# A four-layer graph network kernel: softmax moved down the scheduler's list in the last layer, the layer's end written out, the last output in two pieces

## The chip, the cores and the metric

The kernel runs on one core of a Trainium2 chip. The metric is the device time of one execution in microseconds; several executions were timed and their median is given. One more execution was taken with the hardware profiler; all views and line numbers come from that one.

## The reference

The input x is 128 graphs of 64 nodes with 256 features, float32. Four layers follow each other, each of the form x = x + layer(relu(layernorm(x))). Layers 0 to 2 (two graph convolutions and windows of small LSTMs) are not touched by the change. The last layer is attention over E = 512 edges (src, dst) with 4 heads of 64:

```python
Xq = (H @ W_lin.T).reshape(bt, n, h, dh)
Xv = (H @ W_val.T).reshape(bt, n, h, dh)
e = jnp.einsum('behd,hd->beh', jax.nn.leaky_relu(Xq[:, src] + Xq[:, dst], 0.2), a)
e = e + jnp.log(A0[src, dst] + EPS)[None, :, None]
# softmax of e over the edges of one src node: minus segment_max, exp, over segment_sum
Y = jax.ops.segment_sum(attn[..., None] * Xv[:, dst], src, num_segments=n)
return Y @ W_out.T
```

## The kernel before, in words

The 8192 rows (128 graphs x 64 nodes) stand in SBUF as 16 blocks X[0] to X[15] of 512 rows. The last layer works in groups of four graphs: 32 groups, g = 0 to 31, two groups to a block. Edges are sorted by src and kept as one-hot matrices, so that gathers and segment sums become matmuls: ed_S (src plus dst, one-hot), OST (src, transposed) and ODT (dst, transposed). Eight groups share one score tile "acc" of 128 x 512 (128 rows of graph and head, 512 edges), so softmax is made once for eight groups, after g = 7, 15, 23 and 31.

The steps, with the names that the profile shows:

- turned (L2473): normalizes a block (norm), transposes it on TensorE (ps<-ident,h) and copies the two halves out (hT), one on VectorE, one on ScalarE.
- queries (L2483): four matmul chains hT x (W_lin | W_val), each into one PSUM buffer "ps" of 512 columns (ps<-w_qv,hT). ScalarE copies the first 256 columns out (Q), VectorE the other 256 (XV). Then VectorE forms the linear part of the leaky relu: a product (lin_p) and two reductions (lin).
- score (L2507): eight matmuls Q x ed_S for a group (ps<-ed_S,Q), each into a "ps" buffer, and eight relus on ScalarE (r).
- reduce (L2520): sums r over features with the vector a into acc (acc<-r,ed_apad). The first group of eight starts acc with the log of the adjacency (acc<-ed_log,ones).
- softmax (L2575): calls shifted (L2587): one more matmul adds lin to acc (acc<-ed_S,lin); two scans over the edges give the running maximum per src node from both sides; maximum, subtraction (sm_e), Exp on ScalarE. Then two more scans sum the exponentials per node, with a masking step between them, and a reciprocal and a product give the attention e. All but Exp and the matmul are on VectorE.
- edgewise (L2601), two groups later: transposes e (ps<-ident,sm_e) and copies it into "at".
- between (L2613) calls spread (L2618): four VectorE products at x OST into "aw" buffers (five of them), and gathered (L2629): matmuls aw x ODT into "ps" (ps<-aw,ed_ODT) and one ScalarE copy to "an".
- weighted (L2640): 32 small matmuls an x XV (y<-an,XV) into one PSUM pair of banks, and two copies to "y".
- output (L2656): y x W_out (ps<-w_o,y), VectorE adds it to X (X<-X,ps), and the SyncE queue writes the 256 KB to HBM.
- back (L2227), for g < 8: adds what layer 2 left for a later block (ps<-ident,ls_t).

PSUM in this layer has five "ps" buffers, one "acc" and one pair for y (L2420). Attention runs ten groups behind score (LAG = 10, v = g - 10).

What sets the order: the steps are written in one Python loop (L2434 to L2463), and the tile framework's scheduler lays each engine's instructions out ahead of time. It walks through its own estimate of time and gives an engine, whenever that is free there, the ready instruction that was written first. So the order in the source is a list of priorities and not the order itself. On the chip each engine then takes its instructions in the order laid out. For a group with softmax the list was: score(g), weighted, reduce(g), edgewise, between, **softmax**, turned (next block), back, output, queries (next block). 

The last softmax (q = 3, after g = 31) is written out by hand in turn (L2533): while nc.ordered is set (class Ordered, L788), every instruction on TensorE, VectorE and ScalarE is tied behind the one written before it on the same engine; DMAs are not. In turn, the sums of the exponentials per node come from matmuls with OST (ps<-sm_m,ed_OST), their reciprocals (ed_contr) are spread back by matmuls (ps<-ed_contr,ed_cont), and "at" is the product of the two (at<-sm_m,ps). Groups 22 and 23 are gathered meanwhile, and outputs 20 to 23 made. After turn, a loop (L2465) does between, weighted and output for the last eight groups, with the scheduler choosing the order.

Of the kernel before, what the change touches and what calls it, by code (L numbers as in the profile page):

```python
# [8 lines left out]
F32 = mybir.dt.float32  # L9
# [14 lines left out]
class Ops:  # L24
# [9 lines left out]
    def add(self, o, a, b):  # L34
        self.tt(o, a, b, ALU.add)
# [40 lines left out]
class Eig:  # L76
# [156 lines left out]
    def split(self, D, E):  # L233
# [57 lines left out]
        o.ts(neg[:], ae[:], -1.0, ALU.mult)  # L291
        W, w = t("W", 2), t("w", 1)
        nc.vector.memset(W[:], 0.0)
        for x in range(3):
# [3 lines left out]
            o.mul(ez[:], ez[:], O[:, x, :])  # L298
            col = W[:, 1:2] if x == 1 else W[:, 0:1]
            o.ts(w[:], self.P[:], B1[:, x + 1:x + 2], ALU.is_equal, 0.5 ** 0.5, ALU.mult)  # L300
# [32 lines left out]
        o.stt(self.t("junk4", 4)[:], NB[:], 1.0, self.LM[:], ALU.mult, ALU.mult, acc=n[:])  # L333
        Ws = self.mm(PT[:], W[:])
        WS = t("WS", 2)
# [577 lines left out]
class Fast:  # L913
# [276 lines left out]
    def poly(self, X, each):  # L1190

        o, nc, t = self.o, self.nc, self.t
        PB = t("PB", 128, 33, 64)
        W = t("W", 128, 64)
        o.ts(PB[:, 1, :], X, self.DD[:, 0:1], ALU.subtract)
        for s in range(1, 32):
            o.stt(W[:], X, self.DD[:, s:s + 1], PB[:, s, :], ALU.subtract, ALU.mult)
            o.stt(PB[:, s + 1, :], PB[:, s - 1, :], self.E2[:, s:s + 1], W[:], ALU.mult, ALU.add)
# [244 lines left out]
B, N, D = 128, 64, 256  # L1443
P = 128
# [5 lines left out]
NG = 4  # L1450
# [15 lines left out]
class Kernel:  # L1466
# [949 lines left out]
    def layer3(self):  # L2416
        nc, o, io = self.nc, self.o, self.io
        cx, (w,) = self.stage([("l3x", 1)], "tile")
        with cx:
            cy, pools = self.stage([("l3", 2), ("l3v", 2), ("l3s", 1), ("l3r", 6), ("l3ps", 5), ("l3cps", 1), ("l3yps", 1)], "tile")  # L2420
            with cy:
                self.a02 = self.everywhere(w, "ed_a", io["L3_gnn_a"].rearrange("h d -> (h d)"))
                o.ts(self.a02[:], self.a02[:], 0.2, ALU.mult)
                self.drop, self.dropr = (w.tile([P, E], F32, name="ed_" + n) for n in ("drop", "dropr"))
                o.ts(self.drop[:], self.cont[:], 1.0, ALU.subtract, FLOOR, ALU.mult)
                o.ts(self.dropr[:], self.contr[:], 1.0, ALU.subtract, FLOOR, ALU.mult)
                WQV = w.tile([P, 2, 2 * D], F32, name="w3_qv")
                for x, n in enumerate(("W_lin", "W_val")):
                    nc.sync.dma_start(WQV[:, :, x * D:(x + 1) * D],
                                      io[f"L3_gnn_{n}_t"].rearrange("(k p) m -> p k m", p=P))  # L2430
                WO = self.weights(w, "w3_o", io["L3_gnn_W_out_t"])


                st, LAG = {}, 10  # L2434
                self.turned(st, 0, *pools)
                self.queries(st, 0, WQV, *pools)
                for g in range(8 * NG):
                    v = g - LAG
                    ahead = (g + 1) // 2 if g % 2 and g + 1 < 8 * NG else None
                    self.score(st, g, *pools)  # L2440
                    if v >= 1:
                        self.weighted(st, v - 1, *pools)
                    self.reduce(st, g, *pools)
                    if g % 8 == 1 and 1 < g:
                        self.edgewise(st, g // 8 - 1, *pools)
                    if v >= 0:
                        self.between(st, v, *pools)
                    if g % 8 == 7 and g + 1 < 8 * NG:
                        self.softmax(st, g // 8, *pools)
                    if ahead:  # L2450
                        self.turned(st, ahead, *pools)
                    if g < 8:
                        self.back(8 + g, pools[4], "ps")
                    if g + 6 == 8 * NG:

                        p = pools[4].tile([P, BT], F32, name="ps")
                        for c in range(4):
                            self.nc.tensor.transpose(p[:N, c * P:(c + 1) * P], self.OST[:, c, :], self.ident[:])
                        self.act_copy(self.cont[:N, :], p[:N, :])
                    if v >= 1 and g + 1 < 8 * NG:  # L2460
                        self.output(st, v - 1, WO, *pools)
                    if ahead:
                        self.queries(st, ahead, WQV, *pools)  # L2463
                self.turn(st, WO, pools)
                for v in range(8 * NG - 8, 8 * NG + 2):  # L2465
                    if v < 8 * NG:
                        self.between(st, v, *pools)
                    if 8 * NG - 8 < v <= 8 * NG:
                        self.weighted(st, v - 1, *pools)
                    if v > 8 * NG - 7:  # L2470
                        self.output(st, v - 2, WO, *pools)

    def turned(self, st, i, pool, vp, sp, rp, psum, psc, psy):  # L2473

# [58 lines left out]
    def turn(self, st, WO, pools):  # L2533


        nc, o, psum = self.nc, self.o, pools[4]
        q, v = NG - 1, 8 * NG - 10
        nc.ordered = True
        W = [self.spread(st, v, c, *pools) for c in (0, 2)]
        e, m, m2 = self.shifted(st, q, *pools)  # L2540
        self.output(st, v - 2, WO, *pools)
        self.gathered(st, v, W, *pools)
        et = m2[:].rearrange("p (c b) -> p c b", c=4)
        p = psum.tile([P, 4, P], F32, name="ps")
        for c in range(4):
            nc.tensor.transpose(p[:, c, :], e[:, c * P:(c + 1) * P], self.ident[:])
        self.act_copy(et, p[:])
        self.weighted(st, v - 1, *pools)
        W = [self.spread(st, v + 1, 0, *pools)]
        p = psum.tile([P, P], F32, name="ps")  # L2550
        for c in range(4):
            self.mm(p[:N, :], self.OST[:, c, :], et[:, c, :], c == 0, c == 3)

        sums = self.contr[:N, 0:P]
        o.ts(sums, p[:N, :], 0.5, ALU.max)
        o.recip(sums, sums)
        self.output(st, v - 1, WO, *pools)
        W.append(self.spread(st, v + 1, 2, *pools))
        self.gathered(st, v + 1, W, *pools)
        at = st["at", q] = pools[1].tile([P, 4, 2, 8, 2, HEADS], F32, name="at")  # L2560
        p = psum.tile([P, 4, P], F32, name="ps")
        for c in range(4):
            self.mm(p[:, c, :], self.cont[:N, c * P:(c + 1) * P], sums)
        for x in range(2):
            for m in range(2):
                z = 64 * x + 32 * m
                by = lambda t: t[:, :, z:z + 32].rearrange("p c (a h) -> p c a h", h=HEADS)
                o.mul(at[:, :, x, :, m, :], by(et), by(p))
        self.weighted(st, v, *pools)
        self.output(st, v, WO, *pools)  # L2570
        self.weighted(st, v + 1, *pools)
        nc.ordered = False
        self.output(st, v + 1, WO, *pools)

    def softmax(self, st, q, pool, vp, sp, rp, psum, psc, psy):  # L2575

# [7 lines left out]
        o.mul(e[:], e[:], m2[:])  # L2584
        st["e", q] = e

    def shifted(self, st, q, pool, vp, sp, rp, psum, psc, psy):  # L2587

        nc, o = self.nc, self.o
        acc, lin = st["acc", q], st["lin", q]  # L2590
        self.mm(acc[:], lin[:].rearrange("p x m a h -> p (x m a h)"), self.S2[:], False, True)
        e, m, m2 = (vp.tile([P, E], F32, name="sm_" + x, bufs=1) for x in ("e", "m", "m2"))
        scan = nc.vector.tensor_tensor_scan
        scan(m[:], self.drop[:], acc[:], -FLOOR, op0=ALU.add, op1=ALU.max)
        scan(m2[:, ::-1], self.dropr[:, ::-1], acc[:, ::-1], -FLOOR, op0=ALU.add, op1=ALU.max)
        o.tt(m[:], m[:], m2[:], ALU.max)
        o.sub(e[:], acc[:], m[:])
        self.act(e[:], e[:], AF.Exp)
        return e, m, m2
# [53 lines left out]
            (self.move if g < 8 * NG - 11 else self.act_copy)(y[:, :, :, x, :].rearrange("p f m s -> p m f s"),  # L2653
                      yp[:, x, 0:4 * N].rearrange("p (m f s) -> p m f s", m=2, f=2))

    def output(self, st, g, WO, pool, vp, sp, rp, psum, psc, psy):  # L2656

        y = st["y", g]
        p = psum.tile([P, 2, D], F32, name="ps")
        for m in range(2):  # L2660
            for f in range(2):
                self.mm(p[:, m, :], y[:, f, m].rearrange("p x s -> p (x s)"), WO[:, f, :], f == 0, f == 1)
        x = self.X[g // 2][:, 2 * (g % 2):2 * (g % 2) + 2, :]
        self.o.add(x, x, p[:])
        out = self.io["out"].rearrange("b n d -> (b n) d")
        self.nc.sync.dma_start(out[2 * g * P:(2 * g + 2) * P, :].rearrange("(t p) d -> p t d", p=P), x)

    def run(self):
        self.begin()
# [54 lines left out]
```

## Time and profile before

| what | value |
|---|---|
| median of 3 runs | 2345.52 us (2345.03 to 2349.55) |
| the profiled execution's own time | 2350.61 us |
| its span, first to last instruction | 2348.8 us |
| TensorE busy | 2298.7 us (98%) |
| VectorE busy | 1590.5 us (68%) |
| ScalarE busy | 1138.2 us (48%) |
| mean granted TensorE clock | 0.994 |
| fourth layer | about 1752 us to the end |
| a plain matmul row of it: ps<-aw,ed_ODT, 128x512 | 512 records, 118.2 us |
| aw product on VectorE, 128x1024 | 1220 ns each, some 1150 from start to start |
| reciprocal of sm_m, 128x512 | 3340 ns each, three of them |

PE is TensorE's matmuls, PEld its weight loads, DVE VectorE, ACT ScalarE, POOL GpSimd, SP SyncE. A float32 matmul is two records. Ends of matmuls are modelled, so the time a block of matmuls takes is best read from its first start to the next block's first start. A bracket at the end of a timeline row gives the idle time of that engine before the row, and what ended it. All rows have the line L799, that of a helper that records the instructions, so rows are told apart by their tiles.

### The profile page before, as it was taken

To read this page: it belongs to the slowest core of one execution; us is meant where nothing else is said; L and a number is where in the kernel's file an instruction comes from. 1 tells how busy PE (TensorE), PEld (TensorE's weight loads), DVE (VectorE), ACT (ScalarE), POOL (GpSimd) and SP (SyncE) were. 2 spreads that over 40 slices of the span, in tenths; PEclk is the share of its full clock that TensorE was granted. 3 is DMA by queue.
4 is the path that set the end of the run, shared out by engine and by line. 5 is a ranking of instruction groups with operands and counts; after the bars stand their busy time and mean duration, and the time that the engine had idled before them with its cause. 6 is when DMAs were issued, how large, how long until landed. Compare 5 with 4: busy or idle time off the path is not lost.

```text
span 2348.8 us, 32636 instructions
## 1 busy us (share of the span) xinstructions
PE 2298.7 (98%) x12173; PEld 1633.1 (70%) x12173; DVE 1590.5 (68%) x3988; ACT 1138.2 (48%) x2503; POOL 2.9 (0%) x26
## 2 busy tenths in 40 slices
PE   7999998999999999999999999999999999999999
PEld 4555446986777788888999998888874444444444
DVE  7877676998447777666767667569655566556457
ACT  4665864654436654444444444347445544334321
POOL 0000000000000000000000000000000000000000
PEclk9999999999999999999999999999999999999999
DMA  5000221130010000001000001000020000000001
GB/s 170 1 1 19 63 60 29 66 89 19 1 36 1 1 19 1 1 1 37 1 1 1 1 8 65 1 1 17 1 72 1 1 5 19 14 15 14 19 19 46
DMA packets 61193, 54.86 MB, mean 23 GB/s; under 512 B 15204, under 2 KB 58853, under 8 KB 61029
## 3 DMA queue, kind: packets, MB, share of 16 engines
q1 hardware_dynamic: 61028, 52.73, 7.3%
q8 instruction: 97, 1.59, 0.3%
q14 instruction: 68, 0.55, 0.1%
HBM read 35.93 MB, written 16.78 MB: 22 GB/s over the span
## 4 chain that ended last, share of the span: by engine, by line
PE 80%; DVE 3%; ACT 1%; issue 0%; DMA 0%; ACTq 0%; DVEq 0%
PE ps L799 69%; PE acc L799 5%; PE pt L799 4%; DVE sm_m L799 1%; PE pe L799 1%; PE y L799 1%; DVE X L799 0%; DVE aw L799 0%; ACT ls_g L799 0%; ACT L799 0%; DMA ls_w<-in_L_gnn_Wih_t_dram 0%; DVE ls_g L799 0%; DVE XV L799 0%; DVE ls_t L799 0%; DVE hT L799 0%
## 5 line engine op out<-in xcount | busy, mean ns | idle before, releaser
L799 ACT ACTIVATE ls_g<-ls_g,ls_b 128x512 f32<-128x512 f32 (+4 forms) x472 | 243.0, 565 | 153.4 <-DVE ls_g L799 151.5
L799 ACT ACTIVATE ls_g<-ps,ls_b 128x256 f32<-128x256 f32 (+3 forms) x268 | 115.4, 470 | 330.4 <-PE ps L799 327.1
L799 PE MATMUL ps<-z,w 128*128 128x512 f32 x512 | 259.0, 630 | 0.9 <-ACT z L799 0.9
L799 DVE TENSOR_TENSOR aw<-at,ed_OST 128x1024 f32<-128x1024 f32 x128 | 149.1, 1220 | 97.4 <-PE ps L799 97.4
L799 PE MATMUL ps<-big,X 128*128 128x176 f32 (+3 forms) x848 | 213.0, 367 | 0.8 <-ACT big L799 0.7
L799 DVE TENSOR_TENSOR ls_g<-ls_z,ps 128x512 f32<-128x512 f32 (+5 forms) x256 | 147.1, 580 | 91.4 <-PE ps L799 90.0
L799 PE MATMUL ps<-ls_tx,X 128*128 128x160 f32 (+2 forms) x960 | 207.1, 327 | 0.6 <-ACT ls_g L799 0.6
L799 PE MATMUL ps<-X,X 128*128 128x160 f32 (+1 forms) x896 | 199.1, 306 | 0.0
L799 PE MATMUL ps<-X,ls_w 128*128 128x256 f32 x640 | 190.5, 379 | 0.0
L799 PEld LDWEIGHTS ps<-ls_tx,X 128*128 128x128 f32 x960 | 161.9, 190 | 15.2 <-DVE X L799 4.9
L799 PEld LDWEIGHTS ps<-big,X 128*128 128x128 f32 x848 | 146.1, 190 | 30.5 <-issue 19.4
L799 DVE TENSOR_TENSOR X<-ls_g 128x1024 f32<-128x1024 f32 (+2 forms) x108 | 117.5, 1088 | 51.1 <-ACT ls_g L799 51.1
L799 ACT ACTIVATE r<-ps 128x512 f32<-128x512 f32 x256 | 129.2, 626 | 43.1 <-PE ps L799 43.1
L799 PEld LDWEIGHTS ps<-X,X 128*128 128x128 f32 x896 | 148.5, 190 | 0.0
L799 PE MATMUL ps<-X,ls_s 128*128 128x256 f32 x480 | 142.3, 379 | 0.0
L799 PEld LDWEIGHTS ps<-z,w 128*128 128x128 f32 x512 | 88.7, 193 | 70.9 <-issue 62.3
L799 PE MATMUL ps<-ls_tx,ls_s 128*128 128x256 f32 x464 | 134.9, 379 | 0.0
L799 PE MATMUL ps<-ls_tx,ls_w 128*128 128x256 f32 x464 | 133.4, 380 | 0.0
L799 PEld LDWEIGHTS ps<-X,ls_w 128*128 128x128 f32 x640 | 121.6, 190 | 16.6 <-DVE X L799 0.3
L799 PE MATMUL ps<-big,ls_w 128*128 128x256 f32 x464 | 132.0, 380 | 0.7 <-ACT ls_z L799 0.7
L799 PE MATMUL ps<-ed_S,Q 64*128 64x512 f32 x512 | 129.6, 617 | 2.3 <-DVE XV L799 2.2
L799 ACT ACTIVATE h<-X,n_m,n_r 128x256 f32<-128x256 f32 x192 | 99.6, 590 | 40.9 <-issue 25.0
(543 smaller groups left out, 4010.4 us busy)
## 6 DMA issues: line engine op xcount, KB each, us to landing
X<-in_x_dram SPq DMA_DIRECT2D x32, 512.0 KB
xs<-X SPq DMA_DIRECT2D x16, 512.0 KB
X<-xs SPq DMA_DIRECT2D x16, 512.0 KB
out_dram<-X SPq DMA_DIRECT2D x32, 256.0 KB
X<-in_L_gnn_Wih_t_dram SPq DMA_DIRECT2D x4, 512.0 KB
ls_w<-in_L_gnn_Wih_t_dram SPq DMA_DIRECT2D x4, 512.0 KB
ls_w<-in_L_gnn_Whh_t_dram SPq DMA_DIRECT2D x4, 512.0 KB
w<-in_L_gnn_W_t_dram SPq DMA_DIRECT2D x2, 512.0 KB
```

The lines of the kernel that those rows point to most:

```text
L799: i = method(*a, **kw)
```

## The change

Four edits, all in the fourth layer. First, the acc matmul of lin moves out of shifted into a step of its own, summed, which stands where softmax stood; softmax itself is now written behind queries. Second, in turn, gathered of group 23 moves behind the matmuls and products that make "at", and the first two aw products of group 24 come ahead of weighted(22). Third, the loop over the last eight groups moves into turn, under nc.ordered, with its order written out: the last two aw products of a group, the add and DMA of the output before the last (late), gathered, the first two aw products of the next group, weighted of the group before, and the matmuls of the output before that. Fourth, output can hand its add and DMA back to be made later, and the last group's output is split into two pieces of 128 rows (two graphs) each, each with its own PSUM buffer, add and DMA.

```diff
@@ layer3
                     if g % 8 == 7 and g + 1 < 8 * NG:
-                        self.softmax(st, g // 8, *pools)
+                        self.summed(st, g // 8, *pools)
                     if ahead:
                         self.turned(st, ahead, *pools)
...
                     if ahead:
                         self.queries(st, ahead, WQV, *pools)
+                    if g % 8 == 7 and g + 1 < 8 * NG:
+                        self.softmax(st, g // 8, *pools)
                 self.turn(st, WO, pools)
-                for v in range(8 * NG - 8, 8 * NG + 2):
-                    if v < 8 * NG:
-                        self.between(st, v, *pools)
-                    if 8 * NG - 8 < v <= 8 * NG:
-                        self.weighted(st, v - 1, *pools)
-                    if v > 8 * NG - 7:
-                        self.output(st, v - 2, WO, *pools)
@@ turn
         W = [self.spread(st, v, c, *pools) for c in (0, 2)]
+        self.summed(st, q, *pools)
         e, m, m2 = self.shifted(st, q, *pools)
...
         W.append(self.spread(st, v + 1, 2, *pools))
-        self.gathered(st, v + 1, W, *pools)
         at = st["at", q] = pools[1].tile([P, 4, 2, 8, 2, HEADS], F32, name="at")
...
                 o.mul(at[:, :, x, :, m, :], by(et), by(p))
+        self.gathered(st, v + 1, W, *pools)
+        W = [self.spread(st, v + 2, 0, *pools)]
         self.weighted(st, v, *pools)
-        self.output(st, v, WO, *pools)
-        self.weighted(st, v + 1, *pools)
+
+        late = lambda: None
+        for v in range(8 * NG - 8, 8 * NG + 2):
+            if v < 8 * NG:
+                W.append(self.spread(st, v, 2, *pools))
+            late()
+            if v < 8 * NG:
+                self.gathered(st, v, W, *pools)
+            if v + 1 < 8 * NG:
+                W = [self.spread(st, v + 1, 0, *pools)]
+            if v <= 8 * NG:
+                self.weighted(st, v - 1, *pools)
+            late = self.output(st, v - 2, WO, *pools, late=True)
+        late()
         nc.ordered = False
-        self.output(st, v + 1, WO, *pools)
@@ softmax, shifted
+    def summed(self, st, q, pool, vp, sp, rp, psum, psc, psy):
+
+        self.mm(st["acc", q][:], st["lin", q][:].rearrange("p x m a h -> p (x m a h)"), self.S2[:], False, True)
+
     def shifted(self, st, q, pool, vp, sp, rp, psum, psc, psy):
-        nc, o = self.nc, self.o
-        acc, lin = st["acc", q], st["lin", q]
-        self.mm(acc[:], lin[:].rearrange("p x m a h -> p (x m a h)"), self.S2[:], False, True)
+        nc, o, acc = self.nc, self.o, st["acc", q]
@@ output
+        parts = []
+        for lo, hi in ((0, 1), (1, 2)) if g == 8 * NG - 1 else ((0, 2),):
+            p = psum.tile([P, 2, D], F32, name="ps")[:, 0:hi - lo, :]
+            for m in range(lo, hi):
+                for f in range(2):
+                    self.mm(p[:, m - lo, :], y[:, f, m].rearrange("p x s -> p (x s)"), WO[:, f, :], f == 0, f == 1)
+            parts.append((p, lo, hi))
+
+        def add():
+            for p, lo, hi in parts:
+                x = self.X[g // 2][:, 2 * (g % 2) + lo:2 * (g % 2) + hi, :]
+                self.o.add(x, x, p)
+                self.nc.sync.dma_start(out[(2 * g + lo) * P:(2 * g + hi) * P, :].rearrange("(t p) d -> p t d", p=P), x)
+
+        if late:
+            return add
+        add()
```

More of the change, by code (lines that the diff above doesn't have):

```diff
@@ L2654, in weighted, with output @@
                       yp[:, x, 0:4 * N].rearrange("p (m f s) -> p m f s", m=2, f=2))
-    def output(self, st, g, WO, pool, vp, sp, rp, psum, psc, psy):
+    def output(self, st, g, WO, pool, vp, sp, rp, psum, psc, psy, late=False):
         y = st["y", g]
[L2659 to L2664, printed above, removed]
-        out = self.io["out"].rearrange("b n d -> (b n) d")
-        self.nc.sync.dma_start(out[2 * g * P:(2 * g + 2) * P, :].rearrange("(t p) d -> p t d", p=P), x)
+        out = self.io["out"].rearrange("b n d -> (b n) d")
+        parts = []
[13 more added lines that the diff above has]
+        add()
     def run(self):
```

## The prediction

> **What bounds the kernel now.** I read the page first, then busy time by stage for the last layer, then the timelines of TensorE (PE) and VectorE (DVE) at the places where the stages are longer than their neighbours. The page's first line says who is short of time.
>
> ```profile
> PE 2298.7 (98%) x12173; PEld 1633.1 (70%) x12173; DVE 1590.5 (68%) x3988; ACT 1138.2 (48%) x2503; POOL 2.9 (0%) x26
> ```
>
> PE is the bound, and the chain of waits agrees (PE 80% of it). So an edit outside PE is worth only what it takes out of PE's gaps. The change touches the fourth layer alone (from about 1752 us). Busy time by stage there (columns: stretch, length, busy us of PE, PEld, DVE, ACT, POOL with instructions, granted PE clock, DMA):
>
> ```profile
> 1814.02:1842.30 28.28, 28.28 (x122) 12.31 (x121) 12.64 (x29) 15.63 (x31) 0.00 (x0) 1.00 0.00 1
> 1838.71:1872.58 33.87, 31.80 (x125) 13.12 (x124) 22.11 (x38) 17.71 (x33) 0.00 (x0) 1.00 0.00 1
> 2081.03:2115.59 34.56, 34.56 (x201) 15.45 (x200) 17.82 (x26) 13.89 (x29) 0.00 (x0) 1.00 0.05 16
> 1969.84:2011.15 41.31, 39.81 (x205) 16.74 (x204) 27.94 (x40) 17.39 (x33) 0.00 (x0) 0.96 0.04 13
> 2115.59:2155.26 39.67, 38.17 (x206) 16.41 (x205) 27.02 (x29) 15.90 (x31) 0.00 (x0) 1.00 0.04 14
> ```
>
> The first and third rows are ordinary pairs of groups: PE has no gap at all. The second, fourth and fifth are the same work plus a softmax (g = 7, 15, 23). They carry two matmul pairs that the ordinary rows don't have (acc<-ed_S,lin, 0.96 us from start to next start, and acc<-ed_log, 1.05): 2.01 us of real work. The rest of the excess is stall: 33.87 - 28.28 - 2.01 = **3.58**; 41.31 - 34.56 - 2.01 = **4.74**; 39.67 - 34.56 - 2.01 = **3.10 us**. What stalls PE at g = 23 stands in the DVE timeline (start, duration):
>
> ```profile
> 2128.93 1.22 DVE L799 TENSOR_TENSOR_SCAN sm_m<-ed_drop,acc 128x512 f32<-128x512 f32 x1
> 2130.06 1.20 DVE L799 TENSOR_TENSOR_SCAN sm_m<-ed_dropr,acc 128x512 f32<-128x512 f32 x1
> 2131.18 0.67 DVE L799 COPY hT<-ps 128x512 f32<-128x512 f32 x1
> ...
> 2138.67 1.22 DVE L799 TENSOR_TENSOR_SCAN sm_m<-ed_contr,sm_m 128x512 f32<-128x512 f32 x1
> 2139.91 3.35 DVE L799 RECIPROCAL sm_m<-sm_m 128x512 f32<-128x512 f32 x1
> 2143.18 0.36 DVE L799 COPY XV<-ps 128x256 f32<-128x256 f32 x1
> ```
>
> and in PE's:
>
> ```profile
> 2131.90 7.13 PE L799 MATMUL ps<-w_qv,hT 128*128 128x512 f32 x16 [0.77 <-DVE hT L799]
> 2138.96 3.91 PE L799 MATMUL ps<-ed_S,Q 64*128 64x512 f32 x14
> 2143.60 1.12 PE L799 MATMUL ps<-ed_S,Q 64*128 64x512 f32 x2 [0.73 <-DVE XV L799]
> ```
>
> Two waits, both on a DVE copy standing behind softmax. First, the hT copy runs after two scans though its transposes were over before the first. Second, the fourth XV copy, which frees one of the five PSUM buffers "ps", runs after the reciprocal; score needs that buffer. The bracketed 0.73 understates the second: score takes 5.69 us from its first start to the next step (2138.96 to 2144.65) against 3.84 in ordinary odd steps, so it costs 1.85.
>
> The other place is the written-out turn at the end:
>
> ```profile
> 2282.26 5.05 PE L799 MATMUL ps<-aw,ed_ODT 128*64 128x512 f32 x16
> 2287.24 1.16 PE L799 MATMUL ps<-ed_contr,ed_cont 64*128 64x128 f32 x8
> 2288.32 0.69 PE L799 MATMUL y<-an,XV 64*64 64x64 f32 x32
> 2289.79 1.99 PE L799 MATMUL ps<-w_o,y 128*128 128x256 f32 x8 [0.78 <-ACT y L799]
> 2291.72 0.69 PE L799 MATMUL y<-an,XV 64*64 64x64 f32 x32
> 2293.19 2.00 PE L799 MATMUL ps<-w_o,y 128*128 128x256 f32 x8 [0.78 <-ACT y L799]
> 2295.11 7.45 PE L799 MATMUL ps<-aw,ed_ODT 128*64 128x512 f32 x32
> ```
>
> Twice an output follows its own y at once and waits for ACT's evacuation, and the first aw block takes 4.98 us to the next start where 3.58 is usual. After 2303 PE is full again, 6.13 us a step. The end:
>
> ```profile
> 2344.64 0.69 DVE L799 TENSOR_TENSOR X<-X,ps 128x512 f32<-128x512 f32 x1 [1.04 <-PE ps L799]
> ```
>
> [...] the 0.36 us copy stands behind the 3.35 us reciprocal. [...] XV copies wait for ACT's Q copy of the same bank (32 waits, 34.0 us), so an XV copy is ready only once its Q is. [...] The trace has such a drop of 3.41 us at 2000.50, just after the g = 15 stalls[...]: acc<-r takes 5.13 us there, 3.48 after g = 23. That is the 1.65 by which the fourth row exceeds the fifth.
>
> **The change, part by part.**
>
> *Softmax behind queries.* Nothing is added or removed; the acc matmul stays (summed), the DVE/ACT chain goes behind turned, back, output and queries in the list. At g = 23 DVE comes free at 2129.0 with hT's transposes done, so hT goes first and ends near 2129.7; PE needs it at 2130.7 (end of the w_o step). The gap goes whole: 1.10 - 0.09 (four y records) + 0.08 (the cut y block) + 0.10 (restart of QV, 7.06 against 6.96) = 1.19. The QV block and all XV copies come 1.1 earlier: the last MM ends near 2137.8, Q near 2138.2, XV ready 2138.3, while the chain reaches its reciprocal no sooner than before (2139.9), since hT, the add and three XV copies stood ahead of it already. XV then has the higher place, so the 1.85 goes too: **3.04** at g = 23 and at g = 15. At g = 7: back block 2.30 against 0.87, 1.43; QV 0.10; score 5.95 against 3.84, 2.11; sum 3.64. Here DVE is idle when acc is ready, so one scan (to 1853.1) still precedes hT: QV at 1853.8 where 1853.5 would be free, 0.3 to 0.4 stays: **3.25**. Sum **9.3**. What becomes late is e: lin_p (1.22) and two reductions (2.44) now pass it, 3.7 us. Its reader, the sm_e transposes, comes at 1880.07 against e at 1867.43 (later groups 19 to 21 us): hidden with over 5 us to spare. Bounds: 0 (reciprocal still ahead) to 9.7.
>
> *The turn.* Steps stay, their order changes: gathered(23) after the cont matmuls, weighted one step ahead of its output. PE's excess now, over 2271.60 to 2307.67: y 0.14 + 0.85 + 0.85, aw 1.40 + 0.22 + 0.34 = 3.80. Afterwards DVE paces it: add at 2282.36 as now, two aw to 2285.33, four at products (0.88) to 2286.1, then aw at 1.15 each from 2286.06. PE: cont 2282.26 to 2283.35; gathered(23) waits 0.25 for its last aw; gathered(24) waits 0.6 for its second aw and 0.5 for its fourth; y and outputs wait for nothing, their ACT copies lie a step back. 1.5 stays: **2.3** gained. Bounds 1.0 (DVE a further 1.3 late) to 3.6.
>
> *The loop written out.* PE's order is what the trace has; DVE has four aw and one add, 4 x 1.15 + 0.68 = 5.3 a step, below PE's 6.13. A waiting add would hold the next aw, but its output ended a step before. Zero; if that cover went, each step would cost DVE's surplus.
>
> *Last output in two pieces.* One more DVE add, PSUM tile and DMA; PE's matmuls are the same. The last add handles 256 columns: nearest row XV copy, 0.36 to 0.42, against 0.69: 0.3. Last add's end to last landing is 2345.33 to 2347.49, of which packets 0.92 for 256 KB; half remains: 0.46. The first piece's issue (0.37 on SP) falls near 2344.2, between others. **0.75**; bounds 0.3 (packets gain nothing) to 0.8.
>
> Sum 9.3 + 2.3 + 0.75 = **12.4 us**. Against the profiled execution, 2350.61 us (span 2348.8 and 1.8 around it), that gives 2338.2; without its clock drop, 2336.6. The median of the runs, 2345.52, is 5.1 below the profiled time, so I don't count the drop there: 2345.5 - 12.4 = **2333.1**.
>
> **The rivals.** *A: the order does not change where it counts.* The list is worked off in the scheduler's own time; if XV isn't ready there when the reciprocal is, the reciprocal still goes first. For it: before the reciprocal of g = 7 lower-placed steps of the next block were let in, XV was not. Then XV ends at the same moment, and the earlier QV only waits longer: softmax gains 0, 2.3 + 0.75 remain: 2342.5. Against it: XV is now 1.1 earlier than the chain. *B: in one or two of the three groups* the reciprocal stays ahead: 2336 to 2340. *C: slower.* Softmax is pushed so far back that e is missing at the sm_e transposes, and PE, in order, stands. Spare is 12.6 us at g = 9 and 19 to 21 later, less the 3 gained; each us beyond it is lost whole. To end over 0.2% slower it must eat 12.4 + 4.7 = 17 us, some 5.7 in each of three groups, so a delay of 15 us at the first and 22 at the others; I count 3.7. Time then from 2350 up.
>
> **How the numbers follow.** A measurement of this kernel can tell about 0.2%, 4.7 us. Forecast 0.62, B 0.13 (both faster), A 0.17 (within), C and the like 0.08. Faster 0.75, same 0.17, slower 0.08. The forecast's own range is 2330 to 2336: all upper bounds (9.7 + 3.6 + 0.8) and a clock drop give 2329.8. To leave out at most 2 in 10 the range reaches A: 2329.8 to 2342.8.
>
> **What would show it.** Right: hT ahead of the second scan, XV ahead of the reciprocal in three groups, score 3.84 us, softmax rows at 36.6 us; no wait of an output on ACT y; a last add near 0.4. Wrong: XV still behind the reciprocal, or PE waiting for sm_e at the transposes, or on aw in the closing steps.

## The result and the profile after

| | this | before, beside it | ratio (95% interval) |
|---|---|---|---|
| first measurement, 5 runs each | 2337.39 us (2336.77 to 2338.24) | 2345.77 us (2345.03 to 2351.05) | 0.9954 (0.9943 to 0.9965) |
| the same kernels again, 6 and 11 runs | 2333.61 us (2330.13 to 2337.68) | 2348.31 us (2344.90 to 2352.22) | 0.9941 (0.9927 to 0.9956) |

The kernel became faster by about half a per cent. The two medians differ by 8.4 us in the first row and by 14.7 in the second; neither is the size of the effect. The times of the kernel before gather near 2345, 2347 and 2350 us, and those of the kernel after reach from 2330.1 to 2338.2. In the profiled executions this spread arises ahead of the last 7000 matmul records before the fourth layer, which take 1314.5 to 1314.7 us in every trace: the first 400 us of the program, which the change doesn't touch, hold a varying number of stretches, of 3.41 or 6.83 us each, in which the granted TensorE clock was 0.50 (half-clock stretches, listed in the last section). The fourth layer can be read apart from them, from the first acc<-ed_log matmul to the end of the span, in two profiled executions of each kernel:

| us | before | before again | after | after again |
|---|---|---|---|---|
| own time of the execution | 2350.61 | 2350.62 | 2336.77 | 2331.36 |
| span | 2348.8 | 2348.8 | 2334.9 | 2329.6 |
| start of the fourth layer | 1752.66 | 1752.66 | 1751.50 | 1746.16 |
| **fourth layer** | **596.15** | **596.17** | **583.42** | **583.41** |
| its half-clock stretches | one, 3.41 | one, 3.41 | none | none |

So the change is worth **12.73 us** in the layer that it edits, the same to 0.03 us in both pairs. Of the 13.9 us between the two spans of the first pair, 1.2 came from the untouched part.

The page's first line of the kernel after: PE is busy for 6.6 us less, 5.9 of them in the fourth layer, although its matmuls are the same. Matmuls at half clock or held up inside a block count as busy for longer: the acc<-r block at the half-clock stretch of before takes 5.13 us from start to next start at a mean granted clock of 0.67, 3.48 at 1.00 at g = 23; score at g = 15 of the kernel after, held up without a gap in PE's busy time, takes 4.73 where 3.84 is usual.

```profile
PE 2292.1 (98%) x12173; PEld 1629.9 (70%) x12173; DVE 1591.3 (68%) x3989; ACT 1138.1 (49%) x2503; POOL 2.9 (0%) x26
```

Busy time by stage in the kernel after, for the three pairs of groups with a softmax (stretch, length, then PE, PEld, DVE, ACT, POOL, granted PE clock, DMA):

```profile
1837.55:1868.67 31.12, 30.57 (x126) 12.63 (x125) 20.15 (x37) 17.82 (x33) 0.00 (x0) 1.00 0.00 1
1965.92:2003.34 37.42, 37.42 (x206) 16.19 (x205) 28.06 (x40) 17.27 (x33) 0.00 (x0) 1.00 0.04 15
2107.78:2144.31 36.53, 36.53 (x206) 16.26 (x205) 26.81 (x29) 15.80 (x31) 0.00 (x0) 1.00 0.04 15
```

Against 33.87, 41.31 and 39.67 these are 2.75, 3.89 and 3.14 shorter. In the second row the clock column went from 0.96 to 1.00: of its 3.89, 1.65 is the half-clock stretch (5.13 against 3.48), so that the stalls gave 2.24. An ordinary pair plus the two matmul pairs of a softmax would be 36.57; the third row is there, the second is 0.85 above.

The order that VectorE now has at g = 23 (its timeline, start and duration; rows between are left out where dots stand):

```profile
2121.12 0.68 DVE L799 COPY hT<-ps 128x512 f32<-128x512 f32 x1
2121.72 1.21 DVE L799 TENSOR_TENSOR_SCAN sm_m<-ed_drop,acc 128x512 f32<-128x512 f32 x1
...
2130.94 0.42 DVE L799 COPY XV<-ps 128x256 f32<-128x256 f32 x1
2131.27 1.21 DVE L799 TENSOR_TENSOR lin_p<-Q,ed_a 128x1024 f32<-128x1024 f32 x1
...
2135.98 3.35 DVE L799 RECIPROCAL sm_m<-sm_m 128x512 f32<-128x512 f32 x1
```

hT stands ahead of both scans, and the last XV copy 5 us ahead of the reciprocal. PE has neither of its two waits there any more: QV starts at 2122.89, when the w_o step is over, and score goes from 2129.85 to 2133.69, 3.84 us.

TensorE's timeline in the turn after the change (to be laid beside that of before, 2282.26 to 2295.11):

```profile
2272.39 3.97 PE L799 MATMUL ps<-aw,ed_ODT 128*64 128x512 f32 x16
2276.28 0.69 PE L799 MATMUL y<-an,XV 64*64 64x64 f32 x32
2276.91 4.78 PE L799 MATMUL ps<-aw,ed_ODT 128*64 128x512 f32 x16
2281.62 0.69 PE L799 MATMUL y<-an,XV 64*64 64x64 f32 x32
2282.24 1.99 PE L799 MATMUL ps<-w_o,y 128*128 128x256 f32 x8
2284.16 3.65 PE L799 MATMUL ps<-aw,ed_ODT 128*64 128x512 f32 x16
```

No output waits for ACT's y. The two aw blocks take 3.89 and 4.71 us from start to next start, where 3.59 is usual: 1.4 us of stall remain. From there on a step takes 6.13 us, as before. From the last acc<-ed_S,lin to PE's last matmul it is 70.79 us (2260.65 to 2331.44) against 73.00. The end, on VectorE:

```profile
2330.62 0.42 DVE L799 TENSOR_TENSOR X<-X,ps 128x256 f32<-128x256 f32 x1 [0.18 <-PE ps L799]
2331.48 0.42 DVE L799 TENSOR_TENSOR X<-X,ps 128x256 f32<-128x256 f32 x1 [0.44 <-PE ps L799]
```

The last add takes 0.42 instead of 0.69 us, and from PE's last matmul to the end of the span there are 3.47 instead of 4.21 us.

### The profile page after: what moved, and what is told of

Same layout as the page of the kernel before. It is cut to its first block, busy times and chain, and to the rows that moved or that the text cites. A ratio compares the mean times of both kernels' runs of the same rounds, so it can differ in the third digit from the quotient of the medians.

```text
span 2334.9 us, 32634 instructions
## 1 busy us (share of the span) xinstructions
PE 2292.1 (98%) x12173; PEld 1629.9 (70%) x12173; DVE 1591.3 (68%) x3989; ACT 1138.1 (49%) x2503; POOL 2.9 (0%) x26
## 4 chain that ended last, share of the span: by engine, by line
PE 81%; DVE 2%; issue 0%; ACT 0%; DMA 0%; ACTq 0%; DVEq 0%
PE ps L799 70%; PE acc L799 5%; PE pt L799 4%; PE pe L799 1%; PE y L799 1%; DVE X L799 0%; ACT ls_g L799 0%; DVE aw L799 0%; DVE sm_m L799 0%; DMA ls_w<-in_L_gnn_Wih_t_dram 0%; DVE ls_g L799 0%; DVE n_st L799 0%; DVE ls_t L799 0%; DVE y L799 0%; DVE at L799 0%
```

## The experiments

Theory 1 is the prediction's: PE's stalls come from the order on VectorE; once hT goes ahead of the scans and XV ahead of the reciprocal, both waits end, and the other parts add their own small gains. Each expectation names what speaks against it. The runs are in three sets. Set one takes the change apart, beside 35 runs of the kernel before.

**before_again**: no edit, to see how far two sets of runs of one kernel agree.

> The kernel before, unchanged, for a second profile. Theory 1 (the change saves 11.0 us of PE stall in the fourth layer, as the two profiles show, and what the medians lack, 8.4 against 11.0, comes from half-clock stretches that fall differently from execution to execution): the ratio is 1.000 within 0.2%, the fourth layer (from acc<-ed_log,ones to the span's end) takes 594.5 us plus what a half-clock stretch in it costs, and any difference of this profile's span from 2348.8 us is found in the count and place of half-clock stretches. Rival (the profile of before was exceptional in the fourth layer itself): the fourth layer takes some 592 us with no half-clock stretch, because the stalls at g = 7, 15, 23 are smaller than 3.58, 3.10 and 3.10 us.

Measured: 2345.77 us (13 runs), ratio 0.9995 (0.9986 to 1.0004). The fourth layer took 596.17 us, the expected 594.5 and 1.65 for its half-clock stretch.

**softmax_only**: the first part alone.

```diff
-                        self.softmax(st, g // 8, *pools)
+                        self.summed(st, g // 8, *pools)
...
                         self.queries(st, ahead, WQV, *pools)
+                    if g % 8 == 7 and g + 1 < 8 * NG:
+                        self.softmax(st, g // 8, *pools)
```

> Softmax behind queries alone; turn, loop and last output as before. Theory 1 (the three parts act each in its own place and add up): stalls at g = 7, 15, 23 fall by 2.75, 2.24 and 3.1 us as in the changed kernel, 8.1 together, the turn still takes 36.1 us, and the time is about 5.5 to 8 us below before. Rival (the reordering of one part is worth less without the other, since a stall removed early comes back at the turn): the turn or the closing steps take 2 us or more longer than before, and the time is within 4 us of before.

Measured: 2335.07 us (5 runs), ratio 0.9945 (0.9933 to 0.9958). Fourth layer 586.32 us, 9.85 less than before_again: the three softmax stretches are 2.76, 3.94 and 3.14 us shorter, turn and end unchanged (72.99 and 4.21). The half-clock stretch in the layer is gone here too, so its end goes with this part of the change. The median is 12 us below the kernel before beside it, more than the 5.5 to 8 that were expected: the expectation counted the stalls alone, and this execution, the median one, has only 2 early half-clock stretches, where both traces of before have 5.

**end_only**: the kernel after with softmax directly behind summed and the last output in one piece, so the turn and the written-out loop alone.

```diff
                         self.summed(st, g // 8, *pools)
+                        self.softmax(st, g // 8, *pools)
...
-                    if g % 8 == 7 and g + 1 < 8 * NG:
-                        self.softmax(st, g // 8, *pools)
...
-        for lo, hi in ((0, 1), (1, 2)) if g == 8 * NG - 1 else ((0, 2),):
+        for lo, hi in ((0, 2),):
```

> Turn and closing loop written out as in the changed kernel, with softmax where it was and the last output in one piece. Theory 1: the stalls at g = 7, 15, 23 stay at 3.6, 3.1 and 3.1 us (plus a half-clock stretch if there is one), the time from the last acc<-ed_S,lin to the last matmul falls from 73.0 to 70.8 us, and the whole is 2.2 us below before, near 2343.5. Rival (the written-out loop itself costs something that the turn's gain hides): the steps after gathered(25) take more than 6.13 us each and the gain is under 1 us.

Measured: 2347.88 us (13 runs), ratio 0.9994 (0.9985 to 1.0003): the times can't tell 2 us apart. The trace can: fourth layer 593.89 us, 2.28 less; from the last acc<-ed_S,lin to PE's end 70.79, as in the kernel after. The half-clock stretch is still there (at 2000.8).

**split_only**: the kernel before with output in two pieces for the last group.

```diff
+        for lo, hi in ((0, 1), (1, 2)) if g == 8 * NG - 1 else ((0, 2),):
+            p = psum.tile([P, 2, D], F32, name="ps")[:, 0:hi - lo, :]
+            for m in range(lo, hi):
```

> The last output in two pieces and nothing else. Theory 1: the time from the last matmul to the span's end falls from 4.2 to 3.5 us, the whole is 0.7 us below before, which a timed comparison can't tell from none. Rival (the second DMA's issue and landing eat the shorter add and transfer): the end stays at 4.1 us or more.

Measured: 2348.49 us (14 runs), ratio 0.9999 (0.9990 to 1.0008); in the trace the tail is 3.46 us against 4.20, and the fourth layer 595.41, 0.76 less. The three parts sum to 9.85 + 2.28 + 0.76 = 12.89; together they gave 12.73 to 12.76. Within 0.2 us they are **additive**, so that each can be judged alone.

Set two asks why the order changed PE's waits as it did; each was timed once.

**ht_on_act**: the kernel before, with the first hT copy on ScalarE in the three blocks behind a softmax. That takes the first wait away and leaves the list as it was.

```diff
-            self.move(hT[:, dc, :], p[:])
+            (self.act_copy if i in (4, 8, 12) else self.move)(hT[:, dc, :], p[:])
```

> The kernel before with softmax at the head of the list as it was, but in the three blocks that meet a softmax (4, 8, 12) both hT copies on ScalarE, so that PE is not held by the scans; in the laid-out order at g = 15 and 23 the reciprocal still stands ahead of the fourth XV copy, at g = 7 it stands behind one more XV copy than before. Theory 1 (rival A's reasoning: as long as XV stands behind the reciprocal, an earlier QV block only waits longer at score): at g = 23 the stall before QV (1.1 us) goes, score grows from 5.69 to about 6.8 us, and the stretch from the score of g = 22 to that of g = 25 stays at 53.1 within 0.3 us. Rival (the two stalls are independent): score stays at 5.7 us and the stretch falls by 1.1 us or more.

Measured: 2350.55 us, against 2345.36 for the kernel before beside it; fourth layer 595.61. Its two groups with equal clocks went different ways. At g = 15 QV came without a gap and score paid for it, 6.61 us instead of 5.69. From score at g = 14 to score at g = 17 it is 52.69 us against 54.72 - 1.65 = 53.07, a gain of only 0.4. VectorE's timeline there:

```profile
1996.77 3.34 DVE L799 RECIPROCAL sm_m<-sm_m 128x512 f32<-128x512 f32 x1
2000.03 0.36 DVE L799 COPY XV<-ps 128x256 f32<-128x256 f32 x1
```

and TensorE's:

```profile
2000.45 1.12 PE L799 MATMUL ps<-ed_S,Q 64*128 64x512 f32 x2 [1.55 <-DVE XV L799]
```

The reciprocal is still ahead of the last XV copy, and nearly all the time won at hT is waited for at XV, as theory 1 had it. At g = 23 the bracket stayed 0.73 and score 5.69, and the stretch fell from 53.07 to 51.79: the gain of 1.28 came through, as the rival had it, and outside the 53.1 that theory 1 expected. But the two waits are not independent there. The softmax chain came forward as well: from acc<-ed_S,lin to the reciprocal it takes 11.48 us instead of 12.77. The reason is on ScalarE. At g = 23 of the kernel before, its Exp stands behind the block's first Q copy,

```profile
2133.92 0.38 ACT L799 ACTIVATE Q<-ps 128x256 f32<-128x256 f32 x1 [2.19 <-PE ps L799]
2134.32 1.28 ACT L799 ACT_TABLE_LOAD   x1
2135.61 0.63 ACT L799 ACTIVATE sm_e<-sm_e 128x512 f32<-128x512 f32 x1
```

and VectorE stands idle until the Exp is done:

```profile
2136.28 1.23 DVE L799 TENSOR_TENSOR_SCAN sm_m<-ed_cont,sm_e 128x512 f32<-128x512 f32 x1 [1.17 <-ACT sm_e L799]
```

In this run the Q copy, and the Exp with it, comes 1.30 us earlier after acc<-ed_S,lin, because QV does; VectorE's idle time falls to 0.47. At g = 15 that idle time was 0.29 in the kernel before, since small steps of the normalization fill it, and the chain came forward by only 0.40 (12.80 to 12.40). So in both groups the gain, 0.4 and 1.28, is what the reciprocal came forward: the last XV copy, and score with it, follows the reciprocal, and an earlier hT brings the reciprocal forward through ScalarE. At g = 7 a half-clock stretch of 6.83 us lies in the way (at 1868.1), and the stretch of before at 2000 is gone; that group tells nothing.

**short_reciprocal**: the kernel before with a reciprocal over 64 of the 512 columns; the others keep their sums, so the attention values are not the reference's.

```diff
-        o.recip(m2[:], m2[:])
+        o.recip(m2[:, 0:64], m2[:, 0:64])
```

> The kernel before with the reciprocal of each inner softmax over 64 of its 512 columns, so the other edges keep their sums instead of the reciprocals (this part of the computation is changed); the order laid out should be close to that of before. Theory 1 (score waits for the XV copy because that stands behind the 3.34 us reciprocal): the reciprocal takes 0.5 to 0.8 us, score at g = 7, 15, 23 falls from 5.95, 5.69, 5.69 to between 3.84 and 4.3 us, the wait for hT before QV stays. Rival (score is slow there because ScalarE is late with the relus after Exp and its table load): score stays above 5.2 us.

Measured: 2341.05 us against 2345.36; fourth layer 591.45. Score after the softmax groups 7, 15, 23: 5.26, 4.53, 4.54 us, instead of 5.95, 5.69, 5.69. VectorE at g = 23:

```profile
2131.54 0.55 DVE L799 RECIPROCAL sm_m<-sm_m 128x64 f32<-128x64 f32 x1
2132.12 0.69 DVE L799 TENSOR_TENSOR sm_e<-sm_e,sm_m 128x512 f32<-128x512 f32 x1
2132.73 0.42 DVE L799 COPY XV<-ps 128x256 f32<-128x256 f32 x1
```

The 3.35 us became 0.55, the product moved ahead of XV, XV came 2.1 us earlier relative to the reciprocal's start, and score gained 1.15. The reciprocal's length is therefore a cause of score's stall at g = 15 and 23. The expected 3.84 to 4.3 was missed in all three groups; at g = 23 the product (0.69) that went ahead of XV too is part of what remains. At g = 7 the gain was only 0.69, and 5.26 is above the rival's 5.2, so that group doesn't decide. The hT wait of 0.77 stayed, as it must.

**softmax_middle**: the first part with softmax listed behind back and output but ahead of queries. hT's place is then that of the kernel after, XV's that of the kernel before.

```diff
-                        self.softmax(st, g // 8, *pools)
+                        self.summed(st, g // 8, *pools)
...
+                    if g % 8 == 7 and g + 1 < 8 * NG:
+                        self.softmax(st, g // 8, *pools)
...
                         self.queries(st, ahead, WQV, *pools)
```

> Softmax behind turned, back and output, but still ahead of queries (so XV does not get the higher place). In the laid-out order hT is ahead of the scans, and at g = 15 and 23 all XV copies are ahead of the reciprocal all the same. Theory 1 (hT's place is what decides: with QV earlier, XV is ready in the scheduler's time before the reciprocal is, whatever its place): stretches at g = 14 to 17 and 22 to 25 within 0.5 us of those with softmax behind queries (50.8 and 49.9), g = 6 to 9 within 1.5 us of 34.95. Rival (the place behind queries is what frees score): score stays at 5.5 us or more at g = 15 and 23. A half-clock stretch near g = 16 is expected only if stalls there stay.

Measured: 2338.44 us against 2345.36; fourth layer 587.58, 1.26 more than softmax_only. Its stages by the same view, from the start of score at g = 7, 15 and 23 to the start of score two groups later:

```profile
1839.72:1867.49 27.77, 26.90 (x102) 10.99 (x101) 20.44 (x37) 16.49 (x30) 0.00 (x0) 1.00 0.00 1
1964.74:2002.16 37.42, 37.42 (x206) 16.20 (x205) 28.04 (x40) 17.30 (x33) 0.00 (x0) 1.00 0.04 15
2106.59:2143.12 36.53, 36.53 (x206) 16.26 (x205) 26.82 (x29) 15.81 (x31) 0.00 (x0) 1.00 0.04 15
```

The second and third rows are those of the kernel after to the hundredth. So at g = 15 and g = 23 the place behind queries does nothing for PE: it is enough that softmax stands behind turned, back and output, so that hT, and with it QV and the last XV, come earlier. (The run doesn't separate turned from the other two.) Only at g = 7 does the place count: the same stretch is 26.51 us in the kernel after, and here the reciprocal (1859.85) stands ahead of the last XV (1863.11) again, with score at 5.57 us instead of 4.30.

Set three is the kernel after once more, beside a version that removes what the traces showed to be left.

**after_again**: no edit.

> The changed kernel once more, beside more runs of the kernel before. Theory 1 (the fourth layer is 12.7 us shorter in every execution, 11.1 of stalls and 1.65 of a half-clock stretch that only the kernels with the stalls at g = 15 show; the rest of the difference between medians comes from half-clock stretches in the first 400 us, which fall independently of the change): fourth layer 583.4 us, no half-clock stretch in it; times in groups near 2331 to 2332.5 and 2336.5 to 2338; ratio of the fast runs 0.9945 to 0.9950. Rival (the true gain is the 8.4 us of the first medians): ratio at 0.9960 or above, or a fourth layer of 587 us.

Measured: 2333.61 us, in the table at the top; fourth layer 583.41 us, with no half-clock stretch in it. The ratio, 0.9941, lies a little below the expected 0.9945 to 0.9950 and away from the rival's 0.9960; the two expected groups of times didn't show (2334.35 and 2334.98 lie between them).

**further**: the kernel after, with the scans and the reciprocal of the sums tied behind the last XV copy, edgewise of g = 9 listed behind softmax, and in the turn the add of one output behind two aw products.

```diff
             o.copy(V[:, j, :], p[:, D:2 * D])
+        st["mark"] = self.nc.vector.last
...
         e, m, m2 = self.shifted(st, q, pool, vp, sp, rp, psum, psc, psy)
+        nc.vector.hold = st["mark"]
...
         o.mul(e[:], e[:], m2[:])
+        nc.vector.hold = None
...
-        self.output(st, v - 1, WO, *pools)
+        late = self.output(st, v - 1, WO, *pools, late=True)
         W.append(self.spread(st, v + 1, 2, *pools))
+        late()
```

> The changed kernel with three more moves, all from what its trace shows: the last two scans, the masking, the reciprocal and the product of an inner softmax are tied behind the last XV copy of the same block; edgewise of g = 9 is listed behind queries, so that hT goes ahead of the four at copies; in turn the two aw products (23, 2) go ahead of the add of output 21. Theory: score at g = 7 and 15 falls from 4.30 and 4.73 to 3.84 us, the wait for hT at g = 9 (0.8 us) goes, the turn gains 0.6 us; together 2.6 to 2.9 us, so the fourth layer takes 580.6 us. Rival (the tied chain ends too late and e, aw or y is then waited for at g = 8 to 10 or 16 to 18): one of these groups gets 1 us or more longer, and the gain is under 1.5 us.

Measured: 2329.91 us (2327.63 to 2335.32, 6 runs) beside 2333.61 for the kernel after and 2348.31 for before; ratio to before 0.9928 (0.9914 to 0.9942). Fourth layer 581.03 us, 2.4 less than the kernel after and a little short of the expected 2.6 to 2.9. Two of its stages:

```profile
1958.46:1994.98 36.52, 36.52 (x205) 16.17 (x204) 26.95 (x39) 17.18 (x33) 0.00 (x0) 1.00 0.05 15
2099.43:2135.95 36.52, 36.52 (x205) 16.18 (x205) 26.27 (x29) 15.79 (x31) 0.00 (x0) 1.00 0.04 15
```

With the sums held back, g = 15 is as short as g = 23, and score is 3.84 us in all three groups. Turn and close take 69.98 us, 0.81 less. Ahead of the last XV copy VectorE now stands idle for 1.36 us at g = 15, where it was busy in the kernel after; PE doesn't notice. Listing edgewise of g = 9 later gave only some 0.2, where 0.8 was expected.

## Why the prediction was right, and where it was not

The forecast was 12.4 us by three terms; the layer gave 12.73, by four:

| term | forecast | measured |
|---|---|---|
| softmax, g = 7, 15, 23 | 3.25, 3.04, 3.04 | 2.75, 2.24, 3.14 |
| turn | 2.3 | 2.2 |
| loop written out | 0 | 0 (6.13 us a step, as before) |
| last output split | 0.75 | 0.74 |
| half-clock stretch at 2000.5 | not counted | 1.65 |

**The hT wait.** Right in all three groups. QV starts without a gap at g = 15 and 23; at g = 7 the one scan that precedes hT leaves 1852.66 against some 1852.35, the 0.3 to 0.4 of the prediction. That work which is ready stays behind other work of its engine is to be seen at g = 23 of the kernel before. The last Q copy is over at 2139.45, and the last XV copy starts at 2143.18, behind the reciprocal. PE is idle for 0.77 and for 0.73 us, while 28 of the group's 32 y<-an,XV records, on the tiles that the first four had used at 2130.80, start only at 2144.65.

**XV ahead of the reciprocal.** Right in three groups, so rival A (gain 0) is out, and B too in the form given, that the reciprocal stays ahead in some. Wrong is the size: "XV then has the higher place, so the 1.85 goes too: 3.04 at g = 23 and at g = 15". Score went to 3.84 only at g = 23; it kept 0.89 at g = 15 (4.73) and 0.46 at g = 7 (4.30). The three groups gave 8.1 us for the forecast 9.3. What is still ahead of the last XV at g = 15 is in VectorE's timeline of the kernel after:

```profile
1988.18 0.40 DVE L799 COPY XV<-ps 128x256 f32<-128x256 f32 x1
1988.50 0.68 DVE L799 SCALAR_TENSOR_TENSOR sm_m<-ed_contr,sm_m 128x512 f32<-128x512 f32 x1
1989.22 1.22 DVE L799 TENSOR_TENSOR_SCAN sm_m<-ed_contr,sm_m 128x512 f32<-128x512 f32 x1
1990.36 0.40 DVE L799 COPY XV<-ps 128x256 f32<-128x256 f32 x1
```

The chain's last two short steps lie between the third and the fourth XV copy, although both are listed behind queries. By the scheduler's rule, the order was fixed in its own estimate of time, in which the fourth XV can't have been ready when VectorE came free; a place in the list chooses among steps that are ready, and keeps nothing back. (This is inferred; no trace shows the scheduler's time.) The run further shows that steps of the chain are the cause: with both scans and the masking step tied behind the last XV, score is 3.84. The prediction had used this very argument for rival A, for the reciprocal, and had not asked it of the scan and the masking step ahead of it. Nor did the place behind queries do what the step claims at g = 15 and 23; by softmax_middle, a place behind output was enough there.

**When the chain reaches its reciprocal.** The prediction says "no sooner than before (2139.9), since hT, the add and three XV copies stood ahead of it already". The outcome holds and the reason doesn't. Before, VectorE stood idle for 1.17 us at g = 23 for the Exp, which follows the first Q copy on ScalarE; so an earlier QV can bring the chain forward, as ht_on_act shows. In the kernel after the reciprocal comes later, 16.66 us after acc<-ed_S,lin instead of 12.77, because lin_p and the two reductions now go ahead of it. For the same reason rival A's gain of 0 was too low: with the reciprocal still ahead, ht_on_act gained 0.4 and 1.28.

**The turn.** Right, with its residual: 0.3 in gathered(23) and 1.1 in gathered(24) were measured; 0.25 and 1.1 had been worked out.

**The last output.** Right in both halves: 0.27 from the add and 0.47 from what follows it, for 0.3 and 0.46.

**The half-clock stretch.** This step failed by a choice: "The median of the runs, 2345.52, is 5.1 below the profiled time, so I don't count the drop there". The 5.1 doesn't speak against the stretch. It stands in all four traces of kernels with both waits at g = 15, split_only among them, whose own time is 2344.42, and those traces differ in the first 400 us; it stands in none of the six traces with the softmax move or with the short reciprocal. So these traces speak for 1.65 us that the change gained and the forecast left out. Whether every execution of the kernel before has it, they don't show. That the sum, 12.4, came so close to 12.73 is in part luck: the 1.65 made up for the 1.2 us that the softmax terms lacked. Without it the layer gained 11.1.

**Rival C**, e too late, is out: at g = 7 e is ready at 1870.76, 5.4 us before the sm_e transposes at 1876.15. It comes 21.1 us after acc<-ed_S,lin instead of 16.6, and 3.7 and 3.9 us later in the other two groups, where the prediction had counted 3.7; the spare time there is 13.3 and 12.2 us. The delay cost nothing.

The first median, 2337.39, was 4.3 us above the forecast, outside its own 2330 to 2336 and inside the times given for rival B; the second was 0.5 above. Neither is the miss or the success of a step: in the first profiled execution the fourth layer began at 1751.50, in the second at 1746.16, and the layer itself differs by 0.01 us. It is the order on VectorE that decides against B, not the time.

## What to carry to other kernels

Where a scheduler lays the order out by a list of priorities, moving work down the list helps only at moments when the better work is ready; what must come later has to be held by a dependence, even if the engine then idles. Ask it of every step ahead of the one that you care about, not of the longest alone, and ask which steps of other engines move with it, as the Exp moved with the Q copy here. And where the medians of a kernel scatter by more than the effect, time the stage that the edit touches, and find out where the scatter lies before you take its difference as noise or as signal.

## What was not expected of the hardware

**A short wait that split a pair cost 0.89 us, with no gap to be seen.** The records of score, 16 for eight matmuls, start in pairs, two matmuls on the two halves of the rows: in the first ten records at g = 23 of the kernel after, the two starts are 10 ns apart and a new pair comes every 0.43 us (0.53 behind the first). Starts of the 16 records at g = 23 of the kernel after, then at g = 15 of it, then at g = 23 of the kernel before:

```
2129.85 .86  2130.38 .39  .81 .82  2131.24 .25  .67 .68  2132.10 .19  .53 .64  .96 2133.17
1987.99 .99  1988.52 .53  .95 .96  1989.38 .38  .81  1990.33  .81 .82  1991.34 .35  .77  1992.20
2138.96 .97  2139.49 .50  .92 .93  2140.35 .36  .78  2141.26 .30 .75 .79  2142.28  2143.60  2144.13
```

In the second row the fifth matmul runs alone (1989.81 and 1990.33): the buffer for its partner came at 1990.76. Alone it took 1.00 us to the next start (1990.81), where the two pairs of matmuls ahead of it took 0.96 and 0.86. No idle time is to be seen, and yet the block is 0.89 longer. In the third row the fifth to seventh start one after the other, some 0.5 apart, and the eighth runs alone behind a gap of 0.73, from 2143.60 to the block's end at 2144.65; the block is 1.85 longer. Where the wait fell between two pairs, the gap was nearly all: 0.40 for 0.46 more at g = 7 of the kernel after, 0.63 for 0.70 at g = 23 of short_reciprocal. So the cost of a wait in this paired step was to be read from the block's length, as the prediction did, not from the bracket.

**Half-clock stretches.** The granted clock in them was 0.50 in the traces of before and after. Up to TensorE's last matmul all have 3.41 or 6.83 us:

| trace | stretches before 400 us, sum | start of the fourth layer | in the fourth layer |
|---|---|---|---|
| before | 5, 23.9 us | 1752.66 | 2000.5 |
| after | 4, 20.5 us | 1751.50 | none |
| softmax_middle | 3, 17.1 us | 1749.07 | none |
| split_only | 2, 13.7 us | 1747.16 | 1995.2 |
| after_again | 2, 10.2 us | 1746.16 | none |
| further | 1, 6.8 us | 1744.72 | none |

The longer they last together, the later the layer starts, in the other five traces too (13.7 us with 1746.96 and 1747.81, 23.9 us with 1752.66 to 1753.14): 8 us of spread in a part whose instructions are the same. In the two traces of before and after the shorter stretches last 3.413 us, and the starts are whole multiples of that apart: 25, 24, 50, 4 and 472 of them in the kernel before, 24, 30 and 45 in the kernel after. Why the number of stretches differs between runs of one kernel is not shown here.

The stretch at 2000.5 begins some 19 us after acc<-ed_S,lin of g = 15, in all four traces that have it, behind waits of PE that sum to under 2 us (0.77 and 0.73 in the kernel before). In the 3.41 us just ahead of it PE was idle for only 0.5 to 0.7 us (0.73 in the kernel before). The four begin at nearly the same point, 18.98 to 19.39 us after acc<-ed_S,lin. The same waits at g = 23 had no stretch in any trace, and ht_on_act had one at g = 7 in its place. What trips it stays open.
